# A two-layer graph network on one core: one TensorE signal for a group of products, gathers that follow ScalarE and VectorE, and fixed PSUM tiles

## The chip, the core and the metric

The kernel runs on one core of one Trainium2 chip. The core has five engines with instruction streams of their own: TensorE (PE in the profile; its weight loads are PEld), VectorE (DVE), ScalarE (ACT), GpSimd (POOL) and SyncE (SP, here the issuer of most DMAs). They meet only at semaphores: an instruction may add to one when it ends, and may wait for a value before it starts. The metric is the device time of one launch in microseconds, all inputs and outputs in HBM, everything in fp32.

## The reference

The graph has 6250 nodes with 128 features and 106250 edges (100000 random ones in both directions and a loop per node), sorted by destination. Two attention layers with two heads run over it, with a batch norm and a relu between them, and a residual and a layer norm behind.

```python
def _transformer_conv(h, edge_attr, src, dst, Wq, bq, Wk, bk, Wv, bv, We, Ws, bs):
    ...
    e = (edge_attr @ We).reshape(-1, H, C)
    kj = k[src] + e
    alpha = jnp.einsum('ehc,ehc->eh', q[dst], kj) / jnp.sqrt(jnp.asarray(C, h.dtype))
    amax = jax.lax.stop_gradient(jax.ops.segment_max(alpha, dst, num_segments=n))
    ex = jnp.exp(alpha - amax[dst])
    den = jax.ops.segment_sum(ex, dst, num_segments=n)
    a = ex / den[dst]
    out = jax.ops.segment_sum((v[src] + e) * a[:, :, None], dst, num_segments=n)
    return out.reshape(n, H * C) + h @ Ws + bs
...
rel_t_enc = jnp.cos(rel_t[:, None] * time_w[None, :] + time_b)
edge_attr = jnp.concatenate([rel_t_enc, msg], axis=-1)
h = _transformer_conv(x, edge_attr, src, dst, Wq1, bq1, Wk1, bk1, Wv1, bv1, We1, Ws1, bs1)
mu = h.mean(axis=0)
var = ((h - mu) ** 2).mean(axis=0)
h = (h - mu) / jnp.sqrt(var + 1e-05) * bn_g + bn_b
h = jax.nn.relu(h)
return _transformer_conv(h, edge_attr, src, dst, Wq2, bq2, Wk2, bk2, Wv2, bv2, We2, Ws2, bs2)
...
x = _layernorm(x + _L0_gnn_ref(x, node_vec, edge_index, ...), axis=-1)
```

An edge has 96 features: 32 cosines of a time difference and a 64-wide message.

## The kernel before

**Tiling.** The sorted edges are cut into 105 chunks of 1024 edges, eight tiles of 128. A chunk's destinations lie in a window of 64 nodes, so with two heads a chunk has 128 (node, head) pairs, one per partition. Keys and values are never formed per edge: the weights are folded into a table per node (`ftab`), and a chunk's scores are products of that table with the turned source rows (L847) and with the turned edge features (L848).

**One chunk.** Eight GpSimd indirect DMAs (L757) gather the source rows into `ff`. `turn_in` turns them on TensorE, four 128x128 transposes into one PSUM bank (`fpx`, L820), and in layer 1 the edge features likewise (`fpe`, L833); ScalarE copies both out (`fft` L828, or L826 with a relu for the first six chunks of layer 2, and `fet` L835). In layer 1 SP then stores `fet`, which layer 2 reads back. `score` multiplies, half a chunk at a time, into a bank `fps`. `lowest` takes the minimum on VectorE (two reductions L854, then `fm` L856); `weigh` takes the exponential on ScalarE (two instructions L862), into `fs`. `turn_weights` turns the weights back (L872, two banks `fppt`), ScalarE copies them to `fpt` (L874), and `gather_sums` adds up weighted rows and edge features in `fpa` (L880, eight products of two passes). `divide` normalises on VectorE (L888 to L891, `fa`), `finish_turn` turns the result (L903, L904 into `fpo`), VectorE copies it (L906, `fat`), `apply` multiplies by the value and edge weights (L913 and L914, in layer 2 L919 and L920), and `finish` adds the skip branch (L931) or, in layer 2, begins the layer norm (L944 on).

**Order.** `conv(0)` and `conv(1)`, the two layers, are loops over rounds under a manual schedule: every engine takes its instructions in the order of the text. Round k fetches chunk k + 4, scores chunk k, turns in chunk k + 1, turns the weights and sums up chunk k - 1, and divides and applies chunk k - 2, so four chunks are under way. On TensorE the order of a round is: first scores of k; weights of k - 1; second scores of k; result of k - 2 turned; first half of k + 1 turned; sums of k - 1; second half of k + 1 turned; apply of k - 2; then other work: tables for the next layer, rows turned for the gathers (L630, L1053), pulled from a generator `extra`.

**Gathers.** `tick(step)` issues the next gather of a queue and ties it to `step`: the gather waits until that instruction has ended. Before, all steps are TensorE's products: the scores, the transposes, three of the products of `gather_sums`, the last of `apply`. `allowed` holds gathers to at most three chunks ahead (four late in layer 1), and the marked extra steps are used only when gathers are to be faster.

**PSUM.** There are eight banks: three for whatever is turned (pool `p_tr`, tag "tr"), three for scores (`p_s`), one for `fpa` and one for `fpo`. They come from tile pools, which hand out a bank when its last use has ended, so the product that starts a bank anew waits for its readers and also for TensorE's own last product in it.

**Signals.** Each instruction whose end somebody waits for adds to its engine's semaphore. A consumer of a group of four transposes waits for the last of the four; a gather tied to another product makes that one signal too.

## Time and profile before

| | us |
|---|---|
| three runs | 2709.10, 2718.91, 2722.89 |
| median | 2718.91 |
| the profiled execution | 2692.01 |
| its span | 2690.2 |
| TensorE busy | 2330.4 |
| GpSimd busy | 1618.3 |
| VectorE busy | 1331.9 |
| ScalarE busy | 1264.9 |

The span is the time from the first to the last instruction of the profiled execution. Layer 1's rounds lie from about 95 to 1360 us, layer 2's from about 1425 to 2680. A row of the time-ordered view has start and duration, engine, line, operation with its output and inputs, and how many instructions were put together; in brackets stands how long the engine had been idle before it and what seems to have released it. "issue" is time in which the profile shows nothing that was waited for. A releaser is a guess from semaphore events, so a list of very mixed releasers for one line is itself a finding.

### The profile page before, as it was taken

The page shows a single profiled execution, that of the slowest core. Times are in us where ns is not written, and L with a number is a line of the kernel's source. Part 1 is how long each engine was busy: PE and PEld are TensorE (multiplying, and loading weights), DVE is VectorE, ACT ScalarE, POOL GpSimd, SP SyncE. Part 2 cuts the span into 40 slices and gives each one's busy share as a digit, 9 for nine tenths or more (in the row PEclk, how much of TensorE's full clock was granted, in tenths as well). Part 3 has the DMA queues.
Part 4 walks back from the last instruction along what each step waited for, and adds up shares of the span by engine and source line. Part 5 has one row for each costly group of instructions (what it writes and reads, how often), then busy time and mean ns, then how long its engine had stood idle before and what let it go on. Part 6 is the DMA issues. An engine that isn't in the chain of part 4 may idle for free. (4 is left out here: it accounts for less than half of the span.)

```text
span 2690.2 us, 40319 instructions
## 1 busy us (share of the span) xinstructions
PE 2330.4 (87%) x11482; PEld 1734.9 (64%) x11482; DVE 1331.9 (50%) x4153; ACT 1264.9 (47%) x2147; POOL 1618.3 (60%) x1701
## 2 busy tenths in 40 slices
PE   5898989899898999888957988888898889988887
PEld 3576767667676767767735666666666666666665
DVE  5566666566566666666535433333333333333233
ACT  3666666565555555545523343443334334333344
POOL 3666666666666666666245666666666666666661
PEclk8999999999999999999969999999999999999998
DMA  6455455545555455545365545555555555544451
GB/s 206 143 167 152 140 160 154 149 136 154 161 154 151 136 160 156 153 135 150 103 171 156 143 148 144 138 155 157 153 152 141 151 157 152 153 138 129 132 135 27
DMA packets 239234, 393.49 MB, mean 146 GB/s; under 512 B 62048, under 2 KB 156892, under 8 KB 235676
## 3 DMA queue, kind: packets, MB, share of 16 engines
q1 hardware_dynamic: 166302, 237.60, 29.7%
q0 software_dynamic: 54144, 112.01, 16.4%
q10 hardware_dynamic: 18558, 41.20, 4.3%
q8 instruction: 97, 1.59, 0.2%
q14 instruction: 133, 1.09, 0.1%
HBM read 274.66 MB, written 112.55 MB: 144 GB/s over the span
## 5 line engine op out<-in xcount | busy, mean ns | idle before, releaser
L757 POOL DMA_INDIRECT ff<-xv_d,fsrcs x840 | 808.3, 962 | 482.2 <-issue 172.9
L757 POOL DMA_INDIRECT ff<-hn_d,fsrcs x792 | 758.5, 958 | 434.2 <-issue 167.5
L880 PE MATMUL fpa<-ff,fpt 128*128 128x225 f32 x3360 | 743.0, 377 | 72.6 <-issue 36.9
L880 PEld LDWEIGHTS fpa<-ff,fpt 128*128 128x128 f32 x3360 | 667.7, 205 | 102.1 <-issue 45.4
L828 ACT COPY fft<-fpx 128x512 f32<-128x512 f32 x408 | 240.1, 589 | 627.6 <-PE fpx L820 144.3
L847 PE MATMUL fps<-fft,ftab 128*128 128x512 f32 x840 | 452.0, 620 | 3.1 <-issue 1.8
L854 DVE TENSOR_REDUCE flow<-fps 128x1 f32<-128x512 f32 x420 | 280.6, 685 | 282.4 <-PE fpa L880 99.0
L874 ACT COPY fpt<-fppt 128x512 f32<-128x512 f32 x420 | 228.5, 584 | 329.9 <-remote 71.6
L820 PE MATMUL fpx<-fident,ff 128*128 128x128 f32 x1680 | 263.5, 281 | 24.0 <-issue 15.8
L872 PEld LDWEIGHTS fppt<-fident,fs 128*128 128x128 f32 x1680 | 195.0, 141 | 134.2 <-issue 121.1
L862 ACT ACTIVATE fs<-fps,fm 128x512 f32<-128x512 f32 x420 | 267.4, 692 | 5.2 <-DVE fm L856 2.4
L820 PEld LDWEIGHTS fpx<-fident,ff 128*128 128x128 f32 x1680 | 202.5, 144 | 61.7 <-issue 43.9
L872 PE MATMUL fppt<-fident,fs 128*128 128x128 f32 x1680 | 224.5, 274 | 18.7 <-issue 15.2
L848 PE MATMUL fps<-fet,ftab 112*128 112x512 f32 x420 | 218.8, 602 | 0.0
L944 DVE SCALAR_TENSOR_TENSOR fres<-fpo,fr 64x128 f32<-64x128 f32 x105 | 29.4, 280 | 378.3 <-PE fps L847 107.0
L848 PE MATMUL fps<-fxT,ftab 112*128 112x512 f32 x420 | 216.0, 595 | 0.0
L847 PEld LDWEIGHTS fps<-fft,ftab 128*128 128x128 f32 x840 | 164.3, 227 | 56.6 <-issue 50.5
L903 PEld LDWEIGHTS fpo<-fident,fa 128*128 128x128 f32 x210 | 29.5, 141 | 254.9 <-issue 194.4
L903 PE MATMUL fpo<-fident,fa 128*128 128x128 f32 x210 | 61.9, 295 | 146.7 <-DVE fa L891 92.4
L848 PEld LDWEIGHTS fps<-fet,ftab 112*128 112x128 f32 x420 | 106.0, 253 | 78.3 <-issue 75.6
L835 ACT COPY fet<-fpe 112x512 f32<-112x512 f32 x210 | 124.3, 592 | 57.5 <-PE fpa L880 13.6
L833 PE MATMUL fpe<-fident,ff 128*112 128x128 f32 x840 | 130.4, 279 | 21.6 <-issue 12.9
(217 smaller groups left out, 2559.2 us busy)
## 6 DMA issues: line engine op xcount, KB each, us to landing
fmsg<-in_edge_attr SPq DMA_DIRECT2D x210, 256.0 KB
et_d<-fet SPq DMA_DIRECT2D x105, 448.0 KB
fxT<-et_d SPq DMA_DIRECT2D x105, 448.0 KB
ftab<-tab_d SPq DMA_DIRECT2D x105, 192.0 KB
tab_d<-fo ACTq DMA_DIRECT2D x13, 1536.0 KB
ff<-xv_d,fsrcs POOLq DMA_INDIRECT x840
enc_d<-fzs SPq DMA_DIRECT2D x105, 128.0 KB
ftab<-tab_d SPq DMA_DIRECT2D x105, 128.0 KB
```

The costliest lines, as they stand in the source:

```text
L757: row = nc.gpsimd.indirect_dma_start(out=ch[k].f[:, t, (1 if c else 0):1 + D], out_offset=None, in_=(h_d if k < RAW else hn_d) if c else p ...
L820: turn = nc.tensor.transpose(px[:, t * P:(t + 1) * P], s.f[:, u * 4 + t, 1:1 + D], ident)
L828: nc.scalar.copy(s.ft[:, u * GE:(u + 1) * GE], px)
L833: turn = nc.tensor.transpose(pe[:EC, t * P:(t + 1) * P], s.f[:, u * 4 + t, 1 + D:], ident)
L835: nc.scalar.copy(s.et[:, u * GE:(u + 1) * GE], pe[:EC])
L847: tick(nc.tensor.matmul(ps, s.tab[:, :, 0], s.ft[:, w], start=True, stop=False))
L848: tick(nc.tensor.matmul(ps, s.tab[:EC, :, 1], s.et[:, w], start=False, stop=True), True)
L854: nc.vector.tensor_reduce(low[:, u:u + 1], s.ps[u], AX.X, OP.min)
L862: nc.scalar.activation(s.s[:, u * GE:(u + 1) * GE], s.ps[u], AF.Exp, bias=s.bias, scale=-1.0)
L872: turn = nc.tensor.transpose(pp[:, t * P:(t + 1) * P], s.s[:, at:at + P], ident)
L874: nc.scalar.copy(s.pt[:, u * GE:(u + 1) * GE], pp)
L880: add = nc.tensor.matmul(s.pa, s.pt[:, t * P:(t + 1) * P], s.f[:, t, 1:1 + D + EW], start=t == 0, stop=t == T - 1)
```

## The change

It has three parts. `join(step)` makes a step wait for the last product of the group in `waiting[0]`, so that TensorE need signal once for the group: the copies of `fpx` and `fpe` wait together, those of the two halves `fpt` together, both reductions of `lowest` and the copy `fat` wait for the last transpose of `finish_turn`, and the second copies of `turn_in` wait for the last product of `apply`. For that the copies are moved to `copy_in`, the second after `apply`, and `finish_turn`'s transposes stand before `lowest` in the text; TensorE's own order stays. The ticks are tied to ScalarE's and VectorE's steps in place of products. And PSUM is eight fixed tiles, taken in turn by `bank`. In layer 1 the DMA that fetches `ftab` is joined too.

```diff
@@ -709,11 +709,20 @@
         work = cs.enter_context(tc.tile_pool(name=f"fwork{c}", bufs=2))
         small = cs.enter_context(tc.tile_pool(name=f"fsmall{c}", bufs=3))
         lnp = cs.enter_context(tc.tile_pool(name="fln", bufs=2)) if c else None
-        p_tr = cs.enter_context(tc.tile_pool(name=f"fp_tr{c}", bufs=3, space=bass.MemoryType.PSUM))
-        p_s = cs.enter_context(tc.tile_pool(name=f"fp_s{c}", bufs=3, space=bass.MemoryType.PSUM))
+        p_tr = cs.enter_context(tc.tile_pool(name=f"fp_tr{c}", bufs=1, space=bass.MemoryType.PSUM))
+        p_s = cs.enter_context(tc.tile_pool(name=f"fp_s{c}", bufs=1, space=bass.MemoryType.PSUM))
         p_a = cs.enter_context(tc.tile_pool(name=f"fp_a{c}", bufs=1, space=bass.MemoryType.PSUM))
         p_o = cs.enter_context(tc.tile_pool(name=f"fp_o{c}", bufs=1, space=bass.MemoryType.PSUM))
-        pl.bank = lambda: p_tr.tile([P, GE], F32, name="fpg", tag="tr")
+        turns = [p_tr.tile([P, GE], F32, name=f"ftr{i}") for i in range(3)]
+        scores = [p_s.tile([P, GE], F32, name=f"fps{i}") for i in range(3)]
+        fpa = p_a.tile([P, D + EW], F32, name="fpa")
+        fpo = p_o.tile([P, 2, P], F32, name="fpo")
+
+        def bank(of):
+            of.append(of.pop(0))
+            return of[-1]
+
+        pl.bank = lambda: bank(turns)
 
         together = mybir.DependencyInfo(mybir.DependencyClass.Sync, mybir.DependencyReason.DATA)
         ets = [pl.xT[:EC, i * CE:(i + 1) * CE] for i in range(AHEAD + 2)]
@@ -740,7 +749,9 @@
                 nc.vector.tensor_scalar(f[:, :, D + EW:D + EW + BITS], bits, 0.0, None, op0=OP.is_equal)
                 nc.vector.tensor_copy(f[:, :, D + EW + BITS:], bits)
             s.tab = load.tile([P, NN * H, 3 - c], F32, name="ftab")
-            nc.sync.dma_start(s.tab, pl.tab_d[c][:, bass.ds(s.nb, NN)].rearrange("p n h w -> p (n h) w"))
+            tab = nc.sync.dma_start(s.tab, pl.tab_d[c][:, bass.ds(s.nb, NN)].rearrange("p n h w -> p (n h) w"))
+            if waiting and c == 0:
+                join(tab)
             if c:
                 s.z = load.tile([P, T, TD], F32, name="fz", bufs=AHEAD + 1)
                 nc.sync.dma_start(s.z, enc_d[k].rearrange("p (t d) -> p t d", d=TD))
@@ -765,6 +776,12 @@
         def tick(step, extra=False):
             if queue and queue[0][0] <= allowed[0] and (allowed[1] or not extra):
                 gather(step)
+
+        waiting = []
+
+        def join(step):
+            tc.add_manual_dep(step.ins, waiting[0].ins.name, together, reason="one signal for a group of products")
+            return step
 
         shape = [P, T, TD]
 
@@ -815,24 +832,28 @@
                 if c == 0:
                     s.et = work.tile([EC, CE], F32, name="fet")
             assert u or len(s.rows) == T
-            px = p_tr.tile([P, GE], F32, name="fpx", tag="tr")
+            s.px = bank(turns)
             for t in range(4):
-                turn = nc.tensor.transpose(px[:, t * P:(t + 1) * P], s.f[:, u * 4 + t, 1:1 + D], ident)
+                turn = nc.tensor.transpose(s.px[:, t * P:(t + 1) * P], s.f[:, u * 4 + t, 1:1 + D], ident)
                 for row in s.rows:
                     tc.add_manual_dep(turn.ins, row.ins.name, together, reason="all rows of a chunk are awaited at once")
                 s.rows = []
-            tick(turn, u == 1)
+            if c == 0:
+                s.pe = bank(turns)
+                for t in range(4):
+                    turn = nc.tensor.transpose(s.pe[:EC, t * P:(t + 1) * P], s.f[:, u * 4 + t, 1 + D:], ident)
+            waiting[:] = [turn]
+
+        def copy_in(k, u):
+            s = ch[k]
+            r = slice(u * GE, (u + 1) * GE)
             if c and k < RAW:
-                nc.scalar.activation(s.ft[:, u * GE:(u + 1) * GE], px, AF.Relu, bias=pl.shift, scale=pl.scale)
+                tick(join(nc.scalar.activation(s.ft[:, r], s.px, AF.Relu, bias=pl.shift, scale=pl.scale)))
             else:
-                nc.scalar.copy(s.ft[:, u * GE:(u + 1) * GE], px)
+                tick(join(nc.scalar.copy(s.ft[:, r], s.px)), c == 0)
             if c:
                 return
-            pe = p_tr.tile([P, GE], F32, name="fpe", tag="tr")
-            for t in range(4):
-                turn = nc.tensor.transpose(pe[:EC, t * P:(t + 1) * P], s.f[:, u * 4 + t, 1 + D:], ident)
-            tick(turn, True)
-            nc.scalar.copy(s.et[:, u * GE:(u + 1) * GE], pe[:EC])
+            tick(join(nc.scalar.copy(s.et[:, r], s.pe[:EC])))
             if u:
                 nc.sync.dma_start(et_d[k], s.et)
 
@@ -841,46 +862,46 @@
             s = ch[k]
             if u == 0:
                 s.ps = []
-            ps = p_s.tile([P, GE], F32, name="fps")
+            ps = bank(scores)
             s.ps.append(ps)
             w = slice(u * GE, (u + 1) * GE)
-            tick(nc.tensor.matmul(ps, s.tab[:, :, 0], s.ft[:, w], start=True, stop=False))
-            tick(nc.tensor.matmul(ps, s.tab[:EC, :, 1], s.et[:, w], start=False, stop=True), True)
+            nc.tensor.matmul(ps, s.tab[:, :, 0], s.ft[:, w], start=True, stop=False)
+            waiting[:] = [nc.tensor.matmul(ps, s.tab[:EC, :, 1], s.et[:, w], start=False, stop=True)]
 
         def lowest(k):
             s = ch[k]
             low = small.tile([P, 2], F32, name="flow")
             for u in range(2):
-                nc.vector.tensor_reduce(low[:, u:u + 1], s.ps[u], AX.X, OP.min)
+                tick(join(nc.vector.tensor_reduce(low[:, u:u + 1], s.ps[u], AX.X, OP.min)), True)
             s.bias = small.tile([P, 1], F32, name="fm")
-            nc.vector.tensor_scalar(s.bias, low[:, 0:1], HIGHEST, low[:, 1:2], op0=OP.min, op1=OP.min)
+            tick(nc.vector.tensor_scalar(s.bias, low[:, 0:1], HIGHEST, low[:, 1:2], op0=OP.min, op1=OP.min))
 
         def weigh(k):
             s = ch[k]
             s.s = work.tile([P, CE], F32, name="fs")
             for u in range(2):
-                nc.scalar.activation(s.s[:, u * GE:(u + 1) * GE], s.ps[u], AF.Exp, bias=s.bias, scale=-1.0)
+                tick(nc.scalar.activation(s.s[:, u * GE:(u + 1) * GE], s.ps[u], AF.Exp, bias=s.bias, scale=-1.0))
 
         def turn_weights(k):
 
             s = ch[k]
             s.pt = work.tile([P, CE], F32, name="fpt")
+            pps = []
             for u in range(2):
-                pp = p_tr.tile([P, GE], F32, name="fppt", tag="tr")
+                pp = bank(turns)
                 for t in range(4):
                     at = u * GE + t * P
                     turn = nc.tensor.transpose(pp[:, t * P:(t + 1) * P], s.s[:, at:at + P], ident)
-                tick(turn, u == 1)
-                nc.scalar.copy(s.pt[:, u * GE:(u + 1) * GE], pp)
+                pps.append(pp)
+            waiting[:] = [turn]
+            for u, pp in enumerate(pps):
+                tick(join(nc.scalar.copy(s.pt[:, u * GE:(u + 1) * GE], pp)), u == 1)
 
         def gather_sums(k):
             s = ch[k]
-            s.pa = p_a.tile([P, D + EW], F32, name="fpa")
+            s.pa = fpa
             for t in range(T):
-                add = nc.tensor.matmul(s.pa, s.pt[:, t * P:(t + 1) * P], s.f[:, t, 1:1 + D + EW], start=t == 0,
-                                       stop=t == T - 1)
-                if t in (1, 4, 7):
-                    tick(add)
+                nc.tensor.matmul(s.pa, s.pt[:, t * P:(t + 1) * P], s.f[:, t, 1:1 + D + EW], start=t == 0, stop=t == T - 1)
 
         def divide(k):
             s = ch[k]
@@ -888,7 +909,7 @@
             nc.vector.tensor_scalar(inv, s.pa[:, D + ED:], 1e-30, None, op0=OP.max)
             nc.vector.reciprocal(inv, inv)
             s.a = small.tile([P, D + EW], F32, name="fa")
-            nc.vector.tensor_scalar(s.a, s.pa, inv, None, op0=OP.mult)
+            tick(nc.vector.tensor_scalar(s.a, s.pa, inv, None, op0=OP.mult))
 
         def normalise(k):
             rows = ch[k].f[:, :, 1:1 + D]
@@ -899,11 +920,14 @@
         def finish_turn(k):
             s = ch[k]
 
-            s.po = p_o.tile([P, 2, P], F32, name="fpo")
+            s.po = fpo
             nc.tensor.transpose(s.po[:, 0], s.a[:, :D], ident)
-            nc.tensor.transpose(s.po[:, 1], s.a[:, EW:], ident)
+            waiting[:] = [nc.tensor.transpose(s.po[:, 1], s.a[:, EW:], ident)]
+
+        def keep_turned(k):
+            s = ch[k]
             s.at = small.tile([P, 2, P], F32, name="fat")
-            nc.vector.tensor_copy(s.at, s.po)
+            tick(nc.vector.tensor_copy(s.at, s.po), True)
 
         def apply(k):
             s = ch[k]
@@ -911,14 +935,14 @@
             if c == 0:
 
                 nc.tensor.matmul(po[:, 0], wv[c], at[:, 0], start=True, stop=False)
-                tick(nc.tensor.matmul(po[:, 0], web[c], at[:, 1], start=False, stop=True))
+                waiting[:] = [nc.tensor.matmul(po[:, 0], web[c], at[:, 1], start=False, stop=True)]
                 return
             at = at.rearrange("p i (n h) -> p i n h", h=H)
             for h in range(H):
                 r = slice(h * C, (h + 1) * C)
                 nc.tensor.matmul(po[:NN, 0, r], at[:, 0, :, h], wv[c][:, r], start=True, stop=False)
                 last = nc.tensor.matmul(po[:NN, 0, r], at[:, 1, :, h], web[c][:, r], start=False, stop=True)
-            tick(last)
+            waiting[:] = [last]
 
         def finish(k):
             s = ch.pop(k)
@@ -928,7 +952,8 @@
                 heads = po[:, 0].rearrange("p (n h) -> p n h", h=H)
                 for h in range(H):
                     r = slice(h * C, (h + 1) * C)
-                    nc.vector.tensor_add(res[r], heads[r, :, h], s.tab[r, ::H, 2])
+                    add = nc.vector.tensor_add(res[r], heads[r, :, h], s.tab[r, ::H, 2])
+                tick(add)
                 nc.sync.dma_start(hT[:, bass.ds(s.nb, NN)], res)
                 return
 
@@ -942,7 +967,7 @@
             res = small.tile([NN, D], F32, name="fres")
             mean = small.tile([NN, 1], F32, name="fmean")
             nc.vector.scalar_tensor_tensor(res, po[:NN, 0], 1.0, s.r, op0=OP.mult, op1=OP.add, accum_out=mean)
-            nc.vector.tensor_scalar(mean, mean, -1.0 / D, None, op0=OP.mult)
+            tick(nc.vector.tensor_scalar(mean, mean, -1.0 / D, None, op0=OP.mult))
             nc.vector.tensor_scalar(y[:, g], res, mean, None, op0=OP.add)
             sq = small.tile([NN, D], F32, name="fsq")
             nc.scalar.activation(sq, y[:, g], AF.Square, accum_out=var[:, g:g + 1])
@@ -986,12 +1011,15 @@
                     divide(k - 2)
                 if on(k):
                     score(k, 1)
+                if on(k - 2):
+                    finish_turn(k - 2)
                 if on(k):
                     lowest(k)
                 if on(k - 2):
-                    finish_turn(k - 2)
+                    keep_turned(k - 2)
                 if on(k + 1):
                     turn_in(k + 1, 0)
+                    copy_in(k + 1, 0)
                 if on(k - 1):
                     gather_sums(k - 1)
                 if on(k):
@@ -1000,6 +1028,8 @@
                     turn_in(k + 1, 1)
                 if on(k - 2):
                     apply(k - 2)
+                if on(k + 1):
+                    copy_in(k + 1, 1)
                 if on(k + 2):
                     settle(k + 2)
                 for j in (k + 2,) if k < SINGLE else (k + 2, k + 3) if k == SINGLE else (k + 3,):
```

## The prediction

> **What bounds the kernel now.** I read first the page's engine table, then a table of stages, then single rounds in the order of time, then the waits.
>
> ```profile
> span 2690.2 us, 40319 instructions
> PE 2330.4 (87%) x11482; PEld 1734.9 (64%) x11482; DVE 1331.9 (50%) x4153; ACT 1264.9 (47%) x2147; POOL 1618.3 (60%) x1701
> ```
>
> TensorE (PE) is the fullest engine, but its ends are modelled, so 87% does not say how much could be had. The stages do; columns are the stretch, its length, then busy time and count of PE, its weight loads, VectorE, ScalarE and GpSimd, the granted clock, DMA share and GB/s:
>
> ```profile
> 0.00:95.00 95.00, 54.94 (x209) 35.67 (x210) 49.90 (x156) 35.25 (x46) 41.17 (x60) 0.85 0.57 180
> 95.00:1360.00 1265.00, 1135.66 (x5766) 879.62 (x5765) 804.99 (x2415) 730.27 (x1079) 775.14 (x806) 0.98 0.50 148
> 1360.00:1425.00 65.00, 41.61 (x142) 25.81 (x140) 22.14 (x35) 20.24 (x27) 29.22 (x31) 0.76 0.65 187
> 1425.00:2680.00 1255.00, 1098.18 (x5368) 793.75 (x5367) 454.77 (x1548) 478.73 (x996) 772.79 (x807) 0.95 0.51 141
> ```
>
> Row 2 is layer 1, row 4 layer 2. Each has 105 chunks, so a round takes 1265/105 = 12.05 us and 1255/105 = 11.95 us. That both are 12, though layer 1 has 398 more products and nearly twice the VectorE work, is the first sign that neither engine's work sets the pace. The second sign is rounds near a layer's end, when all row gathers have been issued. In time order, layer 1 (start, duration, engine, line, operation):
>
> ```profile
> 1316.28 0.27 PE L903 MATMUL fpo<-fident,fa 128*128 128x128 f32 x1
> 1316.39 0.27 PE L904 MATMUL fpo<-fident,fa 128*128 128x128 f32 x1
> 1320.42 0.60 PE L820 MATMUL fpx<-fident,ff 128*128 128x128 f32 x4
> 1321.52 0.39 PE L914 MATMUL fpo<-fat,fwe 128*128 128x128 f32 x2
> 1323.52 1.04 PE L872 MATMUL fppt<-fident,fs 128*128 128x128 f32 x8
> 1324.40 1.08 PE L847 MATMUL fps<-fft,ftab 128*128 128x512 f32 x2
> 1326.18 0.27 PE L903 MATMUL fpo<-fident,fa 128*128 128x128 f32 x1
> 1336.08 0.27 PE L903 MATMUL fpo<-fident,fa 128*128 128x128 f32 x1
> ```
>
> L903 comes once per round: 1326.18 - 1316.28 and 1336.08 - 1326.18 are both 9.90 us, without a gap on PE. Layer 2 (L903 of one stretch: count, shortest/median/longest ns, first and last start):
>
> ```profile
> L903 PE MATMUL fpo<-fident,fa x3: 273/274/300, 2640.3 to 2659.2; 128*128 128x128 f32 x3
> ```
>
> Two rounds in 18.9 us, 9.45 each. So the same program runs 2 us a round faster once the gathers are through. What differs in between is seen in an ordinary round of layer 2:
>
> ```profile
> 1893.39 1.04 PE L872 MATMUL fppt<-fident,fs 128*128 128x128 f32 x8
> 1894.27 1.03 PE L847 MATMUL fps<-fft,ftab 128*128 128x512 f32 x2
> 1895.13 1.02 PE L848 MATMUL fps<-fxT,ftab 112*128 112x512 f32 x2
> 1897.35 0.95 POOL L757 DMA_INDIRECT ff<-hn_d,fsrcs  x1 [0.30 <-issue]
> 1899.75 1.07 ACT L874 COPY fpt<-fppt 128x512 f32<-128x512 f32 x2 [4.10 <-remote]
> 1899.84 0.69 DVE L854 TENSOR_REDUCE flow<-fps 128x1 f32<-128x512 f32 x1 [2.33 <-remote]
> 1899.93 0.95 POOL L757 DMA_INDIRECT ff<-hn_d,fsrcs  x1 [1.63 <-remote]
> 1900.39 2.99 PE L880 MATMUL fpa<-ff,fpt 128*128 128x225 f32 x7 [3.47 <-issue]
> ```
>
> The eight transposes L872 were done at 1894.43, the scores L848 at 1896.15. ScalarE's copy, VectorE's second minimum and the next gather needed nothing else, stood idle (in brackets, with the guess at what ended it: "remote", that is nothing found), and all started within 0.2 us of each other, 5.3 and 3.7 us after their products. PE then lost 3.47 us for want of those copies. With no gathers about, the same kind of signal is prompt (last L920 product ends at 2663.23):
>
> ```profile
> 2662.95 0.28 PE L920 MATMUL fpo<-fwe,fat 128*64 128x64 f32 x2
> 2663.27 0.28 DVE L944 SCALAR_TENSOR_TENSOR fres<-fpo,fr 64x128 f32<-64x128 f32 x1 [2.62 <-PE fpo L920]
> ```
>
> 0.04 us. My reading: while gathers run, TensorE's completion signals reach the waiting engines late and in bursts. The totals fit it; first the groups (busy us, mean ns, then idle before them and its main enders), then the waits (us, times, longest):
>
> ```profile
> L828 ACT COPY fft<-fpx 128x512 f32<-128x512 f32 x408 | 240.1, 589 | 627.6 <-PE fpx L820 144.3
> L874 ACT COPY fpt<-fppt 128x512 f32<-128x512 f32 x420 | 228.5, 584 | 329.9 <-remote 71.6
> L757 POOL DMA_INDIRECT ff<-xv_d,fsrcs x840 | 808.3, 962 | 482.2 <-issue 172.9
> PE fpo L903 <- DVE fa L891: 92.4, 56, 5.2
> PE fpa L880 <- issue: 36.9, 28, 3.5
> PE fpa L880 <- ACT fpt L874: 35.7, 21, 3.5
> ```
>
> ScalarE's idle time is named after whichever product came last, and hardly two names agree. The three PE rows are where lateness ends up on PE: 165 us together. The rest of the loss is what PE does at a lower granted clock after its idle times (0.98 and 0.95 in the stages, where a gather-free stretch such as 1320:1350 has 1.00).
>
> ```profile
> 1320.00:1350.00 30.00, 26.27 (x148) 21.98 (x146) 10.74 (x32) 11.01 (x19) 0.00 (x0) 1.00 0.12 36
> ```
>
> **How far it could go.** Extra products for the tables (L630), not in the quiet rounds, cost at most their busy time, in layer 1 and 2:
>
> ```profile
> 95.00:1360.00 1265.00, 59.99 (x116) 18.17 (x116) 0.98 0.50 148
> 1425.00:2680.00 1255.00, 49.67 (x88) 13.16 (x88) 0.95 0.51 141
> ```
>
> 60/105 = 0.57 and 0.47 us a round, so PE's own floor is 9.90 + 0.57 = 10.47 and 9.45 + 0.47 = 9.92 us. GpSimd's floor is eight gathers of 0.95 + 0.30 us (the 1897.35 row) = 10.0 us. The later floor decides: 10.47 in layer 1, 10.0 in layer 2. Above it lie 1.58 x 105 = 166 and 1.95 x 105 = 205 us, 371 in all. Start, middle and end (95 + 65 + 11 us) I leave alone: little of what changes runs there.
>
> **The change, part by part.**
>
> Fewer signals. Counted in the two programs inside the two layers, PE's semaphore updates go from 3279 to 1236, from 15.6 a round to 5.9. In itself a signal costs PE nothing: the quiet rounds carry the old number of them and run without a gap. What falls is what has to be delivered. If late signals are a queue that is drained in bursts, 38% of the load clears much sooner; if a signal waits for a free moment between gathers whatever stands before it, nothing is won. The bounds are all of the 371 us and none. The 1899.75 rows speak for the queue: signals 2 us apart in age came out together. They do not say how many a burst can hold. I take half, 185 us.
>
> PE's waits on itself. Fixed PSUM tiles drop 728 of 729 of them, and 394 semaphore instructions go (177 before L872, 207 before L903). In flow they were free. After a stall they show: L904 to L820 is 0.11 us in a quiet round, but 0.35 us in the round whose L903 had waited:
>
> ```profile
> 1306.10 0.30 PE L903 MATMUL fpo<-fident,fa 128*128 128x128 f32 x1 [0.81 <-DVE fa L891]
> 1306.23 0.27 PE L904 MATMUL fpo<-fident,fa 128*128 128x128 f32 x1
> 1306.58 0.63 PE L820 MATMUL fpx<-fident,ff 128*128 128x128 f32 x4
> ```
>
> Four such instructions stand there, so 0.06 us each: 0 to 24 us for 394. Those at L903 hide under its wait for VectorE, those at L872 mostly behind busy products; I take 0.
>
> Gathers on ScalarE and VectorE. Still eight a round. These engines' signals are prompt also beside gathers, so GpSimd loses less, and PE's queue has one reader less. Steps come later than the products they follow, but GpSimd has 12 - 10 = 2 us a round to spare and works three chunks ahead. If that cover went, each us by which a round's eight were later would be a us of round. I take 0.
>
> Waits added. (1) Both weight copies L874 now start after all eight transposes: the first is later by four, half of L872's spacing to L847, (1324.40 - 1323.52)/2 = 0.44 us; the second is not. Before L880 stand the scores and L903, so this shows only where L880 stalls already. (2) VectorE's minimum waits for L904, which PE did anyway before it: behind it stand fm, L906 and the place of cosines; ScalarE's Exp waits for fm. From L904's end at 1316.66 to L872 at 1323.52 lie 6.9 us; two reductions, fm and two Exp
>
> ```profile
> L854 DVE TENSOR_REDUCE flow<-fps 128x1 f32<-128x512 f32 x420 | 280.6, 685 | 282.4 <-PE fpa L880 99.0
> L862 ACT ACTIVATE fs<-fps,fm 128x512 f32<-128x512 f32 x420 | 267.4, 692 | 5.2 <-DVE fm L856 2.4
> L856 DVE TENSOR_SCALAR fm<-flow 128x1 f32<-128x1 f32 x210 | 45.0, 214 | 12.4
> ```
>
> need 1.37 + 0.2 + 1.38 = 3.0 us, so 3.9 stay. (3) The second half of turn_in is copied after apply: ready at 1321.91 (L914) instead of 1321.02 (L820). Its bank is wanted by L872's second half at 1323.96, one copy of 0.59 later, so cover shrinks from 2.4 to 1.5 us; behind it on ScalarE stands its twin, the copy of fpe, and the edge store on SP. At zero lateness all three cost 0; a signal over 1.5 us late makes the third cost. The half above is net of that.
>
> Sum: 2692 - 185 = 2507 us on the profiled run. It lies 1.0% under the median, 2718.9/2692.0 = 1.010, so the prediction is 2532 us.
>
> One rule stands against a gain of this size. The Trainium skill, "TensorE: Matmul & The Clock Gate", in "The cost: per-tile semaphore tail", says that completion increments serialize at about 26.3 ns each, and that one on the last tile is enough. By that figure 2043 fewer would be an estimate of 54 us, 2638 on the profiled run. The quiet rounds show no such cost in flow.
>
> **The rivals.**
>
> A. Lateness comes from the gathers, not from the count. For: it ends when they end, as shown, and they stay. Against: different ages in one burst. Gain and added waits near 0: 2692 to 2720, 2719 by the median.
>
> B. Slower: lateness stays and the joined waits expose it. Place: the second turn_in's copies. Cover falls by 0.9 us; where a signal is over 2.4 us late the whole 0.9 is lost, between 1.5 and 2.4 part, and L874 adds 0.44 where it stalls. The shown round had 3.7 and 5.3 us; L828's idle, 627.6/408 = 1.5 us on average, holds waiting for the product too, so its lateness is below that. I price 0.35 us a round: 210 x 0.35 = 74, 2766, or 2794 by the median. It decides where mean lateness stays above about 1.5 us.
>
> C. Lateness vanishes and the floors are met: 2692 - 371 = 2321, 2344 by the median. Then GpSimd bounds layer 2. For: ScalarE's and VectorE's signals already behave so. Against: 5.9 signals are left, and PE still waits for copies of the same length.
>
> D. The change only removes the cost of issuing (0 to 24 us above): 2668 to 2692, 2706 by the median. The estimate by the Trainium skill's page above, 54 us, would make it 2664.
>
> **How the numbers follow.** Forecast 0.45 (own range 2420 to 2640: 80% to 20% of the 371), C 0.18, A 0.10, B 0.22, D 0.05. Half a per cent, 14 us, is about what can be told from nothing. Faster: forecast, C and half of D with a little of A, 0.66. Same: most of A and the rest of D, 0.10. Slower: B and some of A, 0.24. The range 2360 to 2770 leaves out C's lower half and B's upper half.
>
> **What would show it.** Right: layer rounds of 11.0 to 11.3 us, granted clock up in layer 2, L828's idle no longer spread over unrelated products, copies within a few tenths of their group's last product, GpSimd over 64%. Queue wrong: starts still in bursts over 1 us after the product, at the same rounds of 12. B: L872 or L847 waiting on L828, which they hardly do now. C: gathers 0.30 us apart without a wait in layer 2. The half is the weakest step; a floor missed by more than 0.3 us in quiet rounds would upset C.

## The result, and the profile after

The changed kernel takes 2879.78 us (median of 4 runs, 2873.14 to 2882.85) against 2720.35 us for the kernel before in the same setting: 1.0591 times as long, 95% interval 1.0555 to 1.0628. The forecast was 2532 us. The page of the changed kernel and its stages, cut where its layers begin and end (columns as before):

```profile
span 2875.2 us, 39905 instructions
PE 2395.8 (83%) x11482; PEld 1759.2 (61%) x11482; DVE 1335.4 (46%) x4153; ACT 1258.7 (44%) x2147; POOL 1620.1 (56%) x1701
```

```profile
0.00:95.00 95.00, 51.54 (x202) 34.98 (x203) 45.66 (x146) 32.56 (x42) 37.33 (x55) 0.82 0.56 177
95.00:1435.00 1340.00, 1162.71 (x5655) 878.48 (x5653) 801.09 (x2383) 713.55 (x1067) 779.99 (x807) 0.95 0.47 139
1435.00:1495.00 60.00, 37.64 (x154) 25.82 (x152) 18.92 (x55) 12.81 (x19) 16.45 (x17) 0.78 0.39 118
1495.00:2865.00 1370.00, 1143.84 (x5475) 819.92 (x5475) 468.76 (x1563) 498.81 (x1016) 786.36 (x823) 0.93 0.47 134
```

Each engine executes as many instructions as before; GpSimd's share fell from 60% to 56%, where over 64% had been forecast. The loss is in the rounds, and in both layers: 1340 and 1370 us, where 1265 and 1255 stood. What PE waits for in the changed kernel (waits: us, times, longest), and two groups of the copies' and minima's idle time; L853 is the former L828, L894 the former L872, L868 L847, L904 L880, L844 L833, L898 L874, L924 and L925 L903 and L904, L875 L854:

```profile
PE fpa L904 <- ACT fpt L898: 96.6, 56, 3.4
PE ftr L894 <- ACT fft L853: 81.8, 56, 3.5
PE fpo L924 <- DVE fa L912: 59.8, 43, 3.7
PE fps L868 <- ACT fft L853: 33.6, 15, 3.2
PE ftr L844 <- ACT fft L853: 17.9, 8, 3.2
```

```profile
L853 ACT COPY fft<-ftr 128x512 f32<-128x512 f32 x408 | 240.1, 588 | 1018.6 <-remote 518.6
L875 DVE TENSOR_REDUCE flow<-fps 128x1 f32<-128x512 f32 x420 | 270.7, 686 | 425.7 <-PE fpo L925 107.6
```

The waits for the copies of turned rows (81.8 + 33.6 + 17.9 = 133 us) are new (before, L872 and L847 waited for them 2.4 us in all); ScalarE's idle time before those copies went from 627.6 to 1018.6 us, and half of it has no releaser that the profile can name. A round of layer 2 in the order of time shows what that is:

```profile
2804.12 0.94 POOL L768 DMA_INDIRECT ff<-hn_d,fsrcs  x1 [2.41 <-ACT fpt L898]
2805.37 0.99 POOL L768 DMA_INDIRECT ff<-hn_d,fsrcs  x1 [0.30 <-DVE fat L930]
...
2810.04 1.04 PE L894 MATMUL ftr<-fident,fs 128*128 128x128 f32 x8
...
2811.67 0.95 POOL L768 DMA_INDIRECT ff<-hn_d,fsrcs  x1 [0.30 <-issue]
...
2812.92 0.94 POOL L768 DMA_INDIRECT ff<-hn_d,fsrcs  x1 [0.30 <-issue]
...
2813.25 0.27 PE L925 MATMUL fpo<-fident,fa 128*128 128x128 f32 x1
...
2816.05 1.07 ACT L898 COPY fpt<-ftr 128x512 f32<-128x512 f32 x2 [3.86 <-remote]
2816.07 1.29 DVE L875 TENSOR_REDUCE flow<-fps 128x1 f32<-128x512 f32 x2 [3.66 <-remote]
2816.69 3.73 PE L904 MATMUL fpa<-ff,fpt 128*128 128x225 f32 x10 [2.73 <-ACT fpt L898]
2816.90 0.94 POOL L768 DMA_INDIRECT ff<-hn_d,fsrcs  x1 [3.04 <-ACT fpt L898]
```

Eight gathers stand 0.3 us apart from 2804.12 to 2813.86. The transposes L894 ended at 2811.08, the turned result at 2813.52; the copy and the minima start together at 2816.05, 5.0 and 2.5 us later, and 2.2 us after GpSimd ran out of gathers. So signals were late as before, with 1236 of them in place of 3279.

Is it the signal that is late, or the engine that wakes late? The trace also records when TensorE's semaphore was raised. In the round of layer 2 that the prediction shows, six recorded updates stand between 1899.67 and 1899.92 us, 0.04 to 0.06 us apart, and none in the 2.9 us ahead of them; the waiting engines start from 1899.75 us on. It is the signal: over the kernel before, 97% of the late starts come within 0.12 us behind a recorded update.

From here a start of ScalarE or VectorE is counted when its engine was idle by the time the product that it waits for ended, and it is called late when it comes over 0.4 us after that end.

### The profile page after: what moved, and what is told of

It reads as the page before. It is cut to its first block, busy times and chain, and to the rows that moved or that the text cites. A ratio compares the mean times of both kernels' runs of the same rounds, so it can differ in the third digit from the quotient of the medians.

```text
span 2875.2 us, 39905 instructions
## 1 busy us (share of the span) xinstructions
PE 2395.8 (83%) x11482; PEld 1759.2 (61%) x11482; DVE 1335.4 (46%) x4153; ACT 1258.7 (44%) x2147; POOL 1620.1 (56%) x1701
## 3 DMA queue, kind: packets, MB, share of 16 engines
q14 instruction: 132, 1.08, 0.1%
## 5 line engine op out<-in xcount | busy, mean ns | idle before, releaser
L904 PE MATMUL fpa<-ff,fpt 128*128 128x225 f32 x3360 | 736.6, 375 | 96.8 <-ACT fpt L898 96.6
L904 PEld LDWEIGHTS fpa<-ff,fpt 128*128 128x128 f32 x3360 | 667.1, 204 | 124.6 <-ACT fpt L898 110.3
L853 ACT COPY fft<-ftr 128x512 f32<-128x512 f32 x408 | 240.1, 588 | 1018.6 <-remote 518.6
L868 PE MATMUL fps<-fft,ftab 128*128 128x512 f32 x840 | 476.0, 650 | 42.0 <-ACT fft L853 33.6
L875 DVE TENSOR_REDUCE flow<-fps 128x1 f32<-128x512 f32 x420 | 270.7, 686 | 425.7 <-PE fpo L925 107.6
L898 ACT COPY fpt<-ftr 128x512 f32<-128x512 f32 x420 | 224.1, 585 | 292.3 <-PE ftr L837 115.7
L894 PEld LDWEIGHTS ftr<-fident,fs 128*128 128x128 f32 x1680 | 198.0, 144 | 242.8 <-ACT fft L853 117.3
L894 PE MATMUL ftr<-fident,fs 128*128 128x128 f32 x1680 | 240.2, 283 | 111.6 <-ACT fft L853 81.8
L837 PE MATMUL ftr<-fident,ff 128*128 128x128 f32 x1680 | 264.5, 282 | 31.4 <-issue 11.6
L883 ACT ACTIVATE fs<-fps,fm 128x512 f32<-128x512 f32 x420 | 266.1, 686 | 23.5 <-DVE fm L877 7.7
L837 PEld LDWEIGHTS ftr<-fident,ff 128*128 128x128 f32 x1680 | 206.5, 145 | 62.7 <-issue 39.1
L868 PEld LDWEIGHTS fps<-fft,ftab 128*128 128x128 f32 x840 | 168.4, 232 | 99.7 <-issue 56.2
L844 PE MATMUL ftr<-fident,ff 128*112 128x128 f32 x840 | 133.4, 283 | 37.8 <-ACT fft L853 17.9
L869 PEld LDWEIGHTS fps<-fxT,ftab 112*128 112x128 f32 x420 | 86.9, 207 | 107.9 <-issue 107.3
L924 PEld LDWEIGHTS fpo<-fident,fa 128*128 128x128 f32 x210 | 30.6, 146 | 191.4 <-DVE fa L912 107.1
L807 DVE SCALAR_TENSOR_TENSOR farg<-fturns,farg 128x256 f32<-128x256 f32 x315 | 134.4, 427 | 10.8
```

Source lines behind the costliest of these rows:

```text
L807: nc.vector.scalar_tensor_tensor(arg, turn, -part, arg, op0=OP.mult, op1=OP.add)
L837: turn = nc.tensor.transpose(s.px[:, t * P:(t + 1) * P], s.f[:, u * 4 + t, 1:1 + D], ident)
L844: turn = nc.tensor.transpose(s.pe[:EC, t * P:(t + 1) * P], s.f[:, u * 4 + t, 1 + D:], ident)
L853: tick(join(nc.scalar.copy(s.ft[:, r], s.px)), c == 0)
L868: nc.tensor.matmul(ps, s.tab[:, :, 0], s.ft[:, w], start=True, stop=False)
L869: waiting[:] = [nc.tensor.matmul(ps, s.tab[:EC, :, 1], s.et[:, w], start=False, stop=True)]
```

## The experiments

**The parts, one at a time.** The gathers alone (the kernel before, with the other ticks moved alike):

```diff
-            tick(turn, u == 1)
...
-                nc.scalar.copy(s.ft[:, u * GE:(u + 1) * GE], px)
+                tick(nc.scalar.copy(s.ft[:, u * GE:(u + 1) * GE], px), c == 0)
...
-                if t in (1, 4, 7):
-                    tick(add)
```

> The kernel before, with the gathers tied to the same ScalarE and VectorE steps as in the changed kernel; no joined waits, pools as before. Theory H (holding): TensorE's signals are held back while gathers run one behind the other, and come when GpSimd pauses. Gathers tied to products are stopped by the late signals themselves and so pause often; tied to ScalarE and VectorE they run in longer rows, and signals come later. Then this part carries most of the loss: 2820 to 2880 us, and late starts in the trace fall into GpSimd's pauses. Rival J (joins): lateness is as before, the joined waits expose it. Then this kernel is near the one before, 2700 to 2740 us.

Measured: 2832.3 us against 2690.05, ratio 1.0543 (1.0486 to 1.0601), as theory H had it. The joins alone (the changed kernel with the old ticks on products):

```diff
-                tick(join(nc.scalar.copy(s.ft[:, r], s.px)), c == 0)
+                join(nc.scalar.copy(s.ft[:, r], s.px))
...
+                if t in (1, 4, 7):
+                    tick(add)
```

> The changed kernel, with the gathers tied to TensorE's products as before; joined waits, moved copies and fixed PSUM tiles stay. Theory H: 2700 to 2770 us, near the kernel before, because gathers pause as they did. Rival J: 2850 to 2890 us, as the changed kernel, with PE idle before L872's and L847's counterparts until the second turn_in's copy.

Measured: 2697.76 us, 1.0024 (1.0009 to 1.0039). The moved gathers carry nearly all. PE's waits with the gathers alone (L898 is the former L903, L870 L872, L845 L847, L832 L833, L827 L828, L886 L891):

```profile
PE fpo L898 <- DVE fa L886: 117.8, 63, 4.8
PE fppt L870 <- ACT fft L827: 97.6, 69, 3.3
PE fps L845 <- ACT fft L827: 42.8, 23, 3.1
PE fpe L832 <- ACT fft L827: 11.8, 6, 3.8
```

The waits for copies of turned rows are all there (152 us) though no wait is joined.

**No gathers at all.** In both kernels the indirect DMAs are replaced by plain ones from SP. They bring rows 128 t on in place of the rows that the edges name, so these kernels leave out the gathering itself; each was executed once:

```diff
-            row = nc.gpsimd.indirect_dma_start(
...
+            row = nc.sync.dma_start(ch[k].f[:, t, (1 if c else 0):1 + D], src[t * P:(t + 1) * P, :])
```

> The kernel before, with each gather replaced by a direct transfer of as many rows and bytes (rows 128 t on, the same for every chunk) issued by SP with the same wait; GpSimd issues nothing in the rounds. Both theories: signals are prompt, rounds go down to the 10.5 and 9.9 us of the floors, 2330 to 2450 us. If signals are late for a reason outside GpSimd's gathers (transfers into SBUF, for one): 2650 us and more.

> The changed kernel with the same replacement of gathers by direct transfers from SP. Both theories: prompt signals make joined waits nearly free, so it is within 2% of the like kernel before (2330 to 2450 us). If the joined waits cost time of their own, without lateness: 60 us or more above it.

Measured: 2614.22 and 2622.8 us, beside 2690.05; without late signals the changed kernel is 0.3% above the other. The total misses the expectation: layer 1 now waits for rows, which SP issues late (338 us of VectorE below). Layer 2 comes within 0.3 us a round of what was expected. Waits of the first kernel, and its turned results in a stretch of layer 2 (L781 is the former L783, L826 L828, L901 L903):

```profile
DVE frel L781 <- DMA ff<-xv_d: 338.1, 70, 8.2
ACT fft L826 <- PE fpx L818: 659.2, 392, 5.6
```

```profile
L901 PE MATMUL fpo<-fident,fa x88: 272/273/302, 1603.3 to 2491.4; 128*128 128x128 f32 x88
```

ScalarE's copies now wait for their own product alone, one name with 392 waits, and a round is 888.1/87 = 10.21 us. Of the starts of ScalarE and VectorE that had to wait for a product, nine in ten are within 0.1 us of it. So in this group of runs signals are late only where GpSimd gathers; as many bytes by plain transfers don't make them late. Whether GpSimd's issuing or the scattered reads do it was not separated.

**Is it the number of signals?** The changed kernel with gathers tied to products that signal anyway, two at a time (one place of several):

```diff
             waiting[:] = [turn]
+            tick(turn)
+            tick(turn)
+            tick(turn, True)
```

> The changed kernel with its gathers tied to the last products of groups that signal anyway (two each to the transposes of turn_in's first half, of turn_weights and to gather_sums, one each to finish_turn and apply): 1350 TensorE signals in the two layers, against 2654 in the kernel with joins and gathers on all products (2698 us) and 1236 in the changed one. Theory H (gathers that run on hold the signals back; the number of signals is without weight): 2690 to 2750 us, near 2698, a little above where two gathers go at once. Rival Q (a queue that fewer signals empty sooner, the reason of the prediction): under 2660 us. If the changed kernel's loss came from the joins with few signals: 2800 us and more.

Measured: 2754.97 us, 1.0137 (1.0106 to 1.0167): over rival Q's 2660 by far, and 5 us over theory H's range. 1350 signals are no better than 2654 (1.0024), rather worse; two gathers at a time are in this too. The other runs agree: joins alone have 625 signals fewer than before, for 1.0024, and with the gathers alone 2363 of TensorE's instructions signal, against 3306 before (whole programs), for 1.0543. A queue that fewer signals empty sooner, on which the forecast stood, is not seen.

**Is it how gathers follow each other?** The kernel before with its ticks saved up and issued behind apply:

```diff
+                if allowed[0] < 12:
+                    gather(step)
+                else:
+                    held.append(step)
...
+                last = held[-1:]
+                while held:
+                    held.pop()
+                    gather(*last)
```

> The kernel before, with all gathers of a round tied to one TensorE product, the last of apply (from the tenth round on), so that they run one behind the other; signals, waits of other engines and pools as before. Theory H: signals are held for a run of eight, about 10 us, and some 1.5 us more; 2820 us or more. Rival E (it matters that gathers wait for ScalarE and VectorE, not how they follow each other): 2680 to 2730 us.

Measured: 2793.42 us, 1.0275 (1.0242 to 1.0308): the number for theory H is missed by 27 us, that for rival E by more. The signals were not as before here: one product in place of eight carries the gathers, and 2348 instructions signal in place of 3306. The gathers alone, with a pause in every fourth:

```diff
+            if (k * T + t) % 4 == 0 and before:
+                tc.add_manual_dep(row.ins, before[0].ins.name, together, reason="a pause")
```

> The kernel with only the gathers moved to ScalarE and VectorE (2832 us), in which every fourth gather of the queue waits also for the one before it to have landed, so that no run is longer than four. Theory H: lateness falls, 2700 to 2790 us, unless the pauses make GpSimd itself the bound (eight gathers of 1.25 us and two pauses of over 1 us are over 12 us), which the trace would show as gathers that wait for nothing but a landing. Rival E: 2820 to 2850 us.

Measured: 3388.99 us, 1.2475. The pause made GpSimd the bound. Its gathers in the order of time (L758 is the former L757):

```profile
2002.38 0.95 POOL L758 DMA_INDIRECT ff<-hn_d,fsrcs  x1 [4.08 <-DMA ff<-hn_d,fsrcs]
2003.63 0.94 POOL L758 DMA_INDIRECT ff<-hn_d,fsrcs  x1 [0.30 <-issue]
2004.88 0.95 POOL L758 DMA_INDIRECT ff<-hn_d,fsrcs  x1 [0.30 <-ACT fs L864]
2006.13 0.95 POOL L758 DMA_INDIRECT ff<-hn_d,fsrcs  x1 [0.30 <-issue]
2009.47 0.94 POOL L758 DMA_INDIRECT ff<-hn_d,fsrcs  x1 [2.40 <-ACT fft L831]
```

But with runs of four and pauses of over 2 us late starts fell from 40% of those counted to 2%, with gathers tied to the same steps. And half the gathers (every second tile by SP, as above, with the wrong rows and executed once):

> The changed kernel with every second gather replaced by a direct transfer of as many bytes from SP (rows 128 t on). Theory H: runs of at most four and long pauses; layer 2's rounds fall from 12.7 to 10.3 to 11.2 us (10.2 where no gather is left), the whole to 2450 to 2650 us. If any gather in flight holds the signals whatever its neighbours do: over 2750 us.

Measured: 2479.37 us; 4% late; layer 2's rounds 10.18 us, layer 1's 12.0, held up by SP's rows as above. Where in a run of gathers (less than 0.5 us between two) a product ended, and how many of the starts that waited for it were late, over the six kernels above that gather everything without a pause (before, changed, gathers alone, joins alone, group ticks, bunched):

```
gather of the run   1st   2nd   3rd   4th   5th   6th   7th
late               17%   17%   25%   56%   74%   85%   86%
mean wait, us     0.29  0.34  0.57  1.55  2.09  2.99  2.90
```

Up to the third, signals mostly pass; from the fifth three in four and more are held. 58 to 85% of the late starts fell into the pauses between runs, which are 23 to 28% of the time, mostly 0.9 to 2.1 us after the run's last gather. Gathers in runs of eight or more were 10% in the kernel before and with the joins alone, 43% in the changed kernel, 52% with the gathers alone. Tied to products, a gather whose step's signal is held stops the run that holds it; tied to ScalarE and VectorE, gathers run on. That doesn't order the times alone: the bunched kernel has 92% in such runs and loses less. Nor does the share of late starts, which is 49% before and 46% in the changed kernel; the mean wait of the counted starts does better, if not in strict order. It is 1.05 us before, 1.08 with the joins alone, 1.15 bunched, 1.17 with group ticks, 1.26 in the changed kernel and 1.50 with the gathers alone. Shorter runs and fewer gathers in a microsecond came together in the kernel with pauses and in that with half the gathers, so which of the two lets signals pass is not shown.

**Runs without late signals.** Kernels were run in groups, each on one chip, beside the kernel before. The next group ran on a chip used earlier:

> The kernel before with the fixed PSUM tiles alone: TensorE's 728 waits on itself go, signals (3279) and gathers stay. Prediction: 0 to 24 us less, taken as 0; both theories the same: 2680 to 2725 us. If waits on itself are late like the other engines' waits, over 40 us less.

> The changed kernel, in which each gather waits also for the landing of the gather two before it. A gather lands some 2.7 us after its issue, two take 2.5 us, so this puts a short gap in each place without letting the gathers run dry. Theory H as it now stands (signals pass up to the fourth gather of a run, and then only when the gathers have run dry): short gaps don't help, lateness stays, 2860 us and more. Rival G (any gap of some tenths of a us lets them pass): lateness falls as in the kernel with pauses, below 2800 us unless GpSimd is the bound.

> The kernel before, in which two of eight gathers (the fourth and the eighth of a chunk) are direct transfers from SP. If the gathers, with the pauses that signals need, set the 12 us rounds of the kernel before: six need 7.5 us and the signals pass more often, layer 2's rounds fall to 10.3 to 11.2 us, the whole to 2420 to 2560 us. If lateness is a fixed cost of having gathers: layer 2's rounds over 11.6 us.

There the kernel before took 2326.96 us in 13 runs, on the chip where it had taken 2690.05. Fixed tiles alone (the diff's first hunk): 2325.81, ratio 0.9994 (0.9983 to 1.0006), so 0 as forecast. The window of two (each gather also waits for the landing of the one two before): 3466.88, bound by landings; with no late signal in the group it decides nothing between H and G. Six gathers (tiles 3 and 7 by SP, wrong rows, one execution): 2382.38, slower than with all eight, VectorE waiting for SP's rows; it too can't answer its question here. The changed kernel and the kernel before, on another chip:

> The changed kernel again, beside the kernel before. In the last call the kernel before took 2327 us in all its runs, against 2690 on the same chip and 2720 on another earlier, and the trace of its variant with fixed PSUM tiles had no late signals at all. Theory S: lateness is a condition of the chip that holds for a whole call, and the change only loses where it is present. If the kernel before takes about 2327 us in this call, the changed kernel takes 2310 to 2350 us, within 1%; if it takes 2690 to 2725 us, the changed kernel takes 2840 to 2890 us. Rival: the change costs some 5% of its own in either condition, 2440 us beside 2327.

> The kernel before, for its trace in this call. Theory S: where it takes about 2327 us, no start over 0.4 us after its product and gathers in rows without pauses, rounds near 10.5 us in layer 1 and 10.0 us in layer 2; where it takes 2690 us and more, starts late as before.

Measured: 2366.94 against 2325.1, ratio 1.0185 (1.0161 to 1.0208); the kernel before, for its trace, 2327.8. Neither theory S's 1% nor the rival's 5%. The kernel before in this group, first its page, then the copies and gathers, then L903 in each layer:

```profile
span 2326.0 us, 40319 instructions
PE 2203.5 (95%) x11482; PEld 1693.2 (73%) x11482; DVE 1331.3 (57%) x4153; ACT 1264.8 (54%) x2147; POOL 1616.9 (70%) x1701
...
L757 POOL DMA_INDIRECT ff<-hn_d,fsrcs x792 | 755.0, 953 | 247.4 <-issue 93.6
...
L828 ACT COPY fft<-fpx 128x512 f32<-128x512 f32 x408 | 238.7, 585 | 577.3 <-PE fpx L820 569.3
```

```profile
L903 PE MATMUL fpo<-fident,fa x105: 273/274/301, 94.8 to 1182.8; 128*128 128x128 f32 x105
L903 PE MATMUL fpo<-fident,fa x105: 272/273/360, 1265.0 to 2312.1; 128*128 128x128 f32 x105
```

Nearly all of L828's idle time has one name, its own product. 96% of the gathers are in runs of eight or more, and of 927 starts counted none comes more than 0.42 us after its product; TensorE's semaphore is raised 0.01 us after a product's end. Rounds are 1088.0/104 = 10.46 and 1047.1/104 = 10.07 us. The parts once more, and the minima without their joined wait, on a third chip:

```diff
-                tick(join(nc.vector.tensor_reduce(low[:, u:u + 1], s.ps[u], AX.X, OP.min)), True)
+                tick(nc.vector.tensor_reduce(low[:, u:u + 1], s.ps[u], AX.X, OP.min), True)
```

> The kernel before with the gathers tied to ScalarE's and VectorE's steps, once more, to see it in the condition without late signals. If the kernel before takes about 2325 us in this call: the gathers' steps come later in the round than the products did, so rows arrive later; 0.2 to 1.2% above it if this part carries the changed kernel's remaining 1.85%, within 0.2% if not. If it takes 2690 us and more (late signals): 5% above, as measured.

> The changed kernel with the gathers tied to products, once more. Without late signals: 0.5 to 1.2% above the kernel before if the joined waits (VectorE's minima, which wait for finish_turn) carry part of the 1.85%, within 0.2% if not. With late signals: 0.2%, as measured.

> The changed kernel without the joined wait of VectorE's minima: each waits for its own scores again (1714 TensorE signals in place of 1236). Without late signals: VectorE's idle time before the minima falls from 119 us in layer 1 towards the 91 us of the kernel before; 10 to 25 us less than the changed kernel's 2367 us if that wait puts VectorE behind, within 5 us if the lateness of rows does it. With late signals: within 1% of the changed kernel.

Measured, against 2327.83: gathers 2358.97, 1.0126 (1.0097 to 1.0155); joins 2332.71, 1.0024 (1.0011 to 1.0037); free minima 2367.04, 1.0168 (1.0140 to 1.0196), no gain that can be told from the changed kernel's 1.0185. The joins cost the same quarter of a per cent in both conditions. With the gathers alone, rows come later. VectorE waits for layer 1's rows before it encodes (this instruction waits for the gathers' semaphores alone, so what is put down to "issue" is such a wait too): in the kernel before (the trace above), then with the gathers alone on the third chip:

```profile
DVE frel L783 <- DMA ff<-xv_d,fsrcs: 12.3, 3, 7.6
DVE frel L783 <- issue: 11.2, 10, 3.6
```

```profile
DVE frel L783 <- issue: 75.7, 56, 5.0
DVE frel L783 <- DMA ff<-xv_d,fsrcs: 34.5, 13, 7.6
```

From 23.5 to 110.2 us; with the joins alone it is 20.8. That these waits are the loss is not shown: the profiled execution is 39 us longer, 26 us of it in layer 1's rounds, where PE's listed waits grew by 12 us, and 12 us in layer 2's, which encode nothing.

## Why the prediction was wrong, by its steps

What bounds the kernel. Right in the main: TensorE's signals, late and in bursts while gathers run, set the 12 us rounds in both layers. The floors worked out from quiet rounds, 10.47 and 10.0 us, were met within 0.1 us by the kernel before itself, in a group where signals are prompt (10.46 and 10.07), and rival C's 2321 us (2344 by the median) stands beside 2327.8. It was not the change that brought it there.

"Gathers on ScalarE and VectorE ... I take 0." This is the step that failed: 5.4% where signals are late, 1.3% where they are not. It looked at GpSimd's spare time and the chunks ahead, and called prompt steps a gain. That gathers on prompt steps run on, and that signals are held longer while they do, was not seen, though the row at 1899.93 had a gather held with the others: late signals were also what broke up the runs (10% of the gathers in runs of eight or more where signals are late, 96% in the same kernel where they are not). The cover named, three chunks ahead, was thin as well: in layer 1 VectorE encodes chunk k + 2 in round k while gathers are held to k + 3 (later k + 3 and k + 4), which leaves it one chunk, and it was seen to wait for rows.

"Fewer signals ... I take half, 185 us." Wrong by all of it, and in kind. With 1350 signals the kernel is no faster than with 2654. Signals of different ages in one burst had been read as a queue whose length matters; in the burst shown they follow each other at 0.04 to 0.06 us, so what costs is the 2.9 us ahead of them, not their number. The quiet rounds didn't carry the old number either: two of them in layer 1 have 12 signals each, not 15.6, since no gather is tied in them. That a signal costs PE nothing came out all the same.

"Waits added." Taken at 0 net; measured 0.24%, about 6 us. Rival B named the right place, PE before L872 and L847 waiting for the copies of turned rows, and its sign, but the wrong cause: the gathers alone bring those waits without any joined wait, and joins alone bring no loss of that size. Its 2794 us was 86 too little.

PE's waits on itself: taken at 0, measured 0.9994. The 26.3 ns per signal that the Trainium skill gives ("TensorE: Matmul & The Clock Gate", "The cost: per-tile semaphore tail"; 54 us by the estimate from it) isn't found here as a saving either: in the groups without late signals, the joins save 625 signals and lose 0.24%.

What stays open: why signals are late in one group and not in the next. Three groups of runs had 2690 to 2720 us for the kernel before, three later ones, on three chips, 2325 to 2328, and one chip was in both, so it is neither the kernel nor that chip. One rival was not tried: that recording delays the signals; no time on record is known to be taken without it. Where signals are late, the trace lacks records of the semaphores, of the kernel before half of ScalarE's updates (867 of 1784 are there); in the later group 1765 of 1784 are there, and without gathers, in the early group, all. So the lost records go with the lateness, and which causes which is open. Open too is why the bunched kernel loses less than the gathers alone: the late rows may be part of it, and where in the round a run lies was not tried.

## What to carry to other kernels

A wait that looks like pure delay may also pace other work; before it is moved to a prompter step, ask what will then run back to back, and what will come later. When one line's idle time is spread over many releasers, or has none, compare its starts with its own products before counting anything as saved. A floor read from a quiet stretch is worth having: it told what the kernel can do when the disturbance is gone.

## What the runs showed that was not expected

With gathers in runs of five and more, TensorE's signals reached ScalarE and VectorE 2 to 3 us late on average, in some groups of runs; signals of VectorE to TensorE, in the same traces, took 0.05 to 0.15 us (L903 behind L891). In other groups no signal was late with 96% of gathers in long runs, and the same program took 13.5% less (2327 against 2690 us on one chip). A change of a few per cent should be measured beside its kernel before, on the same chip and close in time, and a prediction from one trace holds for that trace's condition.
